# Fewer blocks with a dispatch of their own at the end of a hybrid attention and mixture-of-experts kernel

## The chip, the cores and the metric

The kernel runs on one core of a Trainium2 chip. The metric is the time of one execution in microseconds (us). Engines are named as in the profile: PE (matrix products; PEld its weight loads), DVE (vector), ACT (scalar), POOL (GpSimd, which also issues the indirect transfers) and SP (which issues most other transfers).

## The reference

The input is x of shape (4, 256, 64, 64) in float32. A first layer adds a local attention over 3x3 pixels. A second layer takes the pixels as tokens, 16384 of them with 256 channels, adds a gated mean over a window of 64 tokens, and then adds a mixture of eight experts of which each token uses two:

```python
x = x + conv_attention(group_norm(x))           # 3x3 neighbourhood
t = to_tokens(x)
t = t + windowed_mean(layer_norm(t))            # gate * x, window 64
# mixture of experts on tokens = layer_norm(t)
probs = softmax(tokens @ router_w.T)
rw, re = top_k(probs, 2); rw = rw / rw.sum(-1)
combine = zeros((N, 8)).at[arange(N)[:, None], re].set(rw)
out = tokens
for e in range(8):
    h = gelu(tokens @ w1[e] + b1[e])
    out = out + combine[:, e:e + 1] * (h @ w2[e] + b2[e])
x = from_tokens(t + out)
```

## The kernel before

**Blocks.** The 16384 tokens are cut into 32 blocks of 512 (`NB`; four rows of 128 each, `NT`). For each block the stages `attend`, `tail` and `produce` compute everything up to the mixture; `tail` leaves the normed tokens in a tile `tok` (pool `w3p`, tag `xl_tok`, three buffers) and the sum so far in a tile that is stored to `out`.

**Dispatch.** `ranks` gives each token and choice a row in a list of its expert in HBM (`rows_in`) and writes it there with indirect transfers on POOL (L1001): eight per block, each of 128 tokens. The first `NS` = 28 blocks are taken in groups (`GROUPS`: thirteen of two blocks, two of one). The last four blocks (`NB - NS`) form a lot of their own, named `APART`.

**Slots.** As soon as a group's rows are there, `experts` takes its full pieces of 256 rows of one expert as *slots*: four per block, less seven of the first group, 105 in all. For a slot SP fetches the rows (L1171, pool `rowp`, seven buffers), ACT copies the expert's first weights, PE transposes (L1195) and makes both products (L1207, L1225), ACT does the GELU, DVE adds the bias and scales (L1229, L1230), and POOL adds the result onto `out` with two accumulating indirect transfers (L1243), called *sums* here. A slot's sums wait until those of the slot before have landed, since one row may be in both. `give_rows` in `add` lets two or three of the waiting row transfers follow each slot's sums in POOL's order; rows that a fetch needs are given before it at the latest. The function `in_turn` fixes this order.

**Units.** What is left, the rests of the lists (`LEFT` = 21 pieces of 128 rows) and the last four blocks' rows (32 pieces), goes through `halves` as 53 *units* of 128 rows. The two kinds alternate as long as there are rests. Each unit is fetched by SP (L1319), transposed (L1334), multiplied (L1344, L1360), biased and scaled by DVE (L1371, L1372; L1364 first makes its row numbers in a tile with four buffers). Its result is then scattered by POOL into a table `sums_a` in HBM with a plain indirect transfer (L1373), one row for each token and choice, so that scatters need no order among themselves. Pieces of rests may also hold rows of earlier blocks; for these a sum onto `out` follows (L1390), again each behind the landing of the one before. `owed` holds sums that are not yet issued: each unit's scatter earns one credit, and a sum goes when its cost is there (1.5 for a unit's sum, 2.0 for one of the last `HELD` = 2 slots' pairs); with the last unit all that remain go.

**The end.** `together` reads, for the last four blocks, both choices' rows from `sums_a` (L1440, 512 KB a read, half by SP, half by ACT), adds them to the held sum on DVE (L1448) and stores it (L749).

**Order.** The main loop runs over the blocks; `follow` advances the slots' stream so that at the end of the blocks' work eleven, seven and three slots are left at fixed points. The last block's eight row transfers are made at once where `ranks` reaches them. Tiles in a pool take its buffers in turn, and a transfer into a buffer waits for its last reader.

Of the kernel before, what the change touches and what calls it, by code (L numbers as in the profile page):

```python
# [46 lines left out]
FP = mybir.dt.float32  # L47
# [5 lines left out]
P = 128  # L53
# [9 lines left out]
def hybrid_block_kernel(ctx: ExitStack, tc: tile.TileContext, ins: dict, out: bass.AP):  # L63
    nc = tc.nc
    x = ins["x"]
    B, C, FW, _ = x.shape
# [4 lines left out]
    NT = TB // P  # L71
    NBI = HW // TB
    NB = B * NBI
    E = ins["w1b"].shape[0]
# [15 lines left out]
    FETCH = 2  # L90
    I32, U32 = mybir.dt.int32, mybir.dt.uint32
    ENG = mybir.EngineType
    NS = NB - 4
    GROUPS = (*[2] * 13, *[1] * 2)
    assert sum(GROUPS) == NS
    first_of = [sum(GROUPS[:k]) for k in range(len(GROUPS))]
    where = [(k, j) for k, n in enumerate((*GROUPS, NB - NS)) for j in range(n)]
# [2 lines left out]
    U = 2  # L100
# [14 lines left out]
    RW = C + 2 * E  # L115
# [640 lines left out]
    def tail(g):  # L756
# [114 lines left out]
        if g < RAMP:  # L871
            scales()
        sent = t2
        if NS <= g < NS + 2:
            sent = xsp.tile([P, NC, TB], FP, tag="xs", name=f"held_{g}")
            sent = sent.rearrange("p c n -> p (c n)").rearrange("p (t c) -> p t c", t=NT)
        at = tc.cur_priority
# [76 lines left out]
    def ranks(g):  # L954
# [34 lines left out]
        def dispatch(inst):  # L989

            for i in range(k + 1):
                tc.declare_no_dep(
                    inst, group=f"dispatch_{i}", reason="no two tokens have one row"
                )
            tc.declare_no_dep(inst, group="fetch", reason="fetched rows are not written again")
            tc.add_to_no_dep_group(f"dispatch_{k}", inst)
            dispatched[k].append(inst)
            return inst
# [8 lines left out]

        for t in range(NT):
            for c in range(2):
                if g == NB - 1:  # L1010
                    dispatch(give(t, c).ins)
                elif g < first_of[2]:
                    waiting.append((k, lambda t=t, c=c: dispatch(paced(give(t, c)).ins)))
                else:
                    waiting.append((k, lambda t=t, c=c: in_turn(
                        dispatch(give(t, c).ins), adds[-1:], given_rows
                    )))
            yield
# [105 lines left out]

    ready = []
    adds = []
    HELD, owed = 2, []
    waiting, given_rows = [], []

    def in_turn(inst, others, own):  # L1130
# [17 lines left out]
    def experts():  # L1148
# [86 lines left out]
        def add(m, xs):  # L1235
            k, n = of[m]

            behind = adds[-U:]
            if n == 0:
                at = 1 + sum(GROUPS[:k])  # L1240
                behind = behind + stored[0 if k == 0 else at : at + GROUPS[k]]
            for t in range(U):
                inst = nc.gpsimd.indirect_dma_start(  # L1243
                    out=out, out_offset=bass.IndirectOffsetOnAxis(
                        ap=xs[:, t, C + E : C + E + 1].bitcast(U32), axis=0
                    ),
                    in_=xs[:, t, 0:C], in_offset=None, compute_op=ALU.add,
                ).ins
                tc.declare_no_dep(
                    inst, group="stores", keep=behind, reason="rows of a later group's blocks"  # L1250
                )
                tc.declare_no_dep(
                    inst, group="adds", keep=behind, reason="behind the slot before, no other"
                )
                for d in behind:
                    tc.add_manual_dep(
                        inst, d.name,
                        mybir.DependencyInfo(
                            mybir.DependencyClass.Sync, mybir.DependencyReason.DATA
                        ),  # L1260
                        reason="sums of one row",
                    )
                tc.add_to_no_dep_group("adds", inst)
                in_turn(inst, given_rows[-2:], [])
                adds.append(inst)
            give_rows(2 + (m % 3 == 0))

        raw = {m: fetch(m) for m in range(FETCH)}
        xcs, hs, done = {}, {}, {}
# [18 lines left out]
    def halves():  # L1288
# [10 lines left out]
            )  # L1299

        xs, w1s, xc, hs = {}, {}, {}, {}
        thirds, halved = [], []
        token = w1p.tile([P, HALVES], U32, tag="token", name="token")
        credit = 0.0

        def fetch(m):
            give_rows(0, APART)
            at = load(m, 1, [ENG.SP], E * ROOM)
            if order[m] < LEFT:
                if len(halved) == 0:  # L1310
                    both = rowp.tile([P, U, RW], FP, tag="xs", name=f"sxl_{m}")
                    halved.extend(both[:, n] for n in range(U))
                xs[m] = halved.pop(0)
            else:
                if len(thirds) == 0:
                    three = xp.tile([P, 3, RW], FP, tag="x", name=f"sxa_{m}")
                    thirds.extend(three[:, n] for n in range(3))
                xs[m] = thirds.pop(0)
            inst = nc.sync.dma_start(xs[m], rows_in[bass.ds(at, P), :]).ins  # L1319
            tc.add_to_no_dep_group("fetch", inst)  # L1320
            for d in dispatched[APART]:
                tc.add_manual_dep(
                    inst, d.name,
                    mybir.DependencyInfo(mybir.DependencyClass.Sync, mybir.DependencyReason.DATA),
                    reason="rows of the slot",
                )
# [27 lines left out]
        def output(m):  # L1354
            nonlocal credit
            e = load(m, 0, [ENG.PE, ENG.DVE], E - 1)
            h, x_ = hs.pop(m), xs.pop(m)
            ps = ps_a.tile([P, C], FP, tag="a", name=f"psya_{m}")
            for f in range(NC):
                nc.tensor.matmul(  # L1360
                    ps, h[:, f, :], w2[:, e, f, :], start=(f == 0), stop=(f == NC - 1)
                )
            to = w4p.tile([P, 1], U32, tag="to", name=f"to_{m}")
            nc.vector.tensor_tensor(  # L1364
                to, x_[:, bass.ds(e + C + E, 1)].bitcast(U32), spare[:, m : m + 1], ALU.max
            )
            if order[m] < LEFT:
                nc.vector.tensor_tensor(
                    token[:, m : m + 1], x_[:, bass.ds(e + C + E, 1)].bitcast(U32), beyond, ALU.min
                )  # L1370
            nc.vector.tensor_add(x_[:, 0:C], ps, b2b[:, e, :])  # L1371
            nc.vector.tensor_scalar_mul(x_[:, 0:C], x_[:, 0:C], x_[:, bass.ds(e + C, 1)])  # L1372
            inst = nc.gpsimd.indirect_dma_start(  # L1373
                out=sums_a[:, :], out_offset=bass.IndirectOffsetOnAxis(ap=to[:, 0:1], axis=0),
                in_=x_[:, 0:C], in_offset=None,
            ).ins
            tc.declare_no_dep(inst, group="sums", reason="one row for each token and choice")
            tc.add_to_no_dep_group("sums", inst)
            given_rows.append(inst)
            in_turn(inst, adds[-1:], [])  # L1380
            if order[m] < LEFT:
                owed.append((1.5, lambda: add(m, x_)))
            credit = credit + 1.0 if owed else 0.0
            while owed and (credit >= owed[0][0] or m == HALVES - 1):
                cost, sum_ = owed.pop(0)
                sum_()
                credit -= cost
# [33 lines left out]
    def together():  # L1421

        part = NT // 2
        for g in range(NS, NB):
            sums_of = None
            for n in range(0, NT, part):
                if g == NB - 1:
                    both = w3p.tile([P, NT, RW], FP, tag="xl_tok", name=f"both_{g}_{n}")
                    both = both.rearrange("p t r -> p (t r)")[:, 0 : 2 * part * C]
                    both = both.rearrange("p (t k c) -> p t k c", k=2, c=C)  # L1430
                elif g == NB - 2:
                    both = w2p.tile([P, NT, C + 1 + E], FP, tag="wx", name=f"both_{g}_{n}")
                    both = both.rearrange("p t r -> p (t r)")[:, 0 : 2 * part * C]
                    both = both.rearrange("p (t k c) -> p t k c", k=2, c=C)
                else:
                    if n == 0:
                        sums_of = xpp.tile([P, NT, 2, C], FP, tag="xp", name=f"both_{g}")
                    both = sums_of[:, n : n + part]
                first = OWN + 2 * ((g - NS) * TB + n * P)
                (nc.scalar if n else nc.sync).dma_start(  # L1440
                    both,
                    sums_a[first : first + 2 * part * P, :].rearrange(
                        "(t p k) c -> p t k c", p=P, k=2
                    ),
                )
                own = held[g][:, n : n + part]
                for k in range(2):
                    nc.vector.tensor_add(own, own, both[:, :, k, :])  # L1448
                store(g, own, n)
# [119 lines left out]
```

## Time and profile before

| what | value |
|---|---|
| median of three runs | 1240.46 us (1238.21 to 1243.04) |
| the profiled execution | 1240.63 us |
| its span, first to last instruction | 1238.9 us |
| PE, DVE, ACT, POOL busy | 90%, 74%, 69%, 57% of the span |
| row transfers L1001 | 256 of 0.995 us on average, 84.3 to 1056.8 us |
| slots' sums L1243 | 210 of 1.594 us, 188.0 to 1094.0 us |
| units' scatters L1373 | 53 of 0.96 us (median), 1082.4 to 1216.4 us |
| units' sums L1390 | 21 of 1.594 us (median), 1098.9 to 1200.0 us |
| reads of `sums_a` L1440 | 8 of 512 KB, from 1218.9 us |

Times on POOL are those of issuing the transfer; the transfer itself lands later. The idle time before an instruction is shown in brackets with what ended it. Of PE's products the ends are modelled, so its rows overlap a little.

### The profile page before, as it was taken

What the parts mean: (1) busy time and instruction counts of PE and PEld (TensorE: products, weight loads), DVE (VectorE), ACT (ScalarE), POOL (GpSimd) and SP (SyncE); (2) the same over time, 40 slices, a digit from 0 to 9 for tenths busy, and PEclk for the clock granted to TensorE, in tenths of its full rate; (3) what the DMA queues carried; (4) which work ended last, traced back from release to release, by engine and by line L of the source; (5) the groups of instructions that cost most, each with busy time, mean ns of one, the idle gap of its engine ahead of it and who ended that gap; (6) DMA issues with size and microseconds to landing.
All of it is one profiled execution on the core that took longest, in us unless ns stands there. A gap on an engine that the chain in (4) does not pass through costs nothing. (4 is left out here: it accounts for less than half of the span.)

```text
span 1238.9 us, 28986 instructions
## 1 busy us (share of the span) xinstructions
PE 1111.5 (90%) x8762; PEld 792.2 (64%) x8762; DVE 913.7 (74%) x4632; ACT 857.3 (69%) x1752; POOL 700.9 (57%) x642
## 2 busy tenths in 40 slices
PE   5988889999998979999999999999999999676882
PEld 3544456677675756777677666766766677565771
DVE  4589878888886867887988877888888887233344
ACT  1566679878886768787787787877877774344561
POOL 4013325666553655666655766665756577566671
PEclk7999999999998989999999999999999999889996
DMA  9894547666767667777766777766665456655446
GB/s 284 269 314 157 186 136 224 194 159 155 177 164 157 162 181 192 198 194 198 187 168 159 177 188 177 181 169 166 166 166 101 99 121 151 130 139 127 101 104 233
DMA packets 136145, 214.00 MB, mean 173 GB/s; under 512 B 16368, under 2 KB 102400, under 8 KB 131768
## 3 DMA queue, kind: packets, MB, share of 16 engines
q1 hardware_dynamic: 86264, 137.00, 35.8%
q0 software_dynamic: 48352, 73.05, 29.5%
q10 hardware_dynamic: 1376, 2.10, 0.5%
q8 instruction: 73, 1.20, 0.4%
q14 instruction: 80, 0.66, 0.2%
HBM read 120.78 MB, written 91.31 MB: 171 GB/s over the span
## 5 line engine op out<-in xcount | busy, mean ns | idle before, releaser
L1243 POOL DMA_INDIRECT out<-sx x210 | 334.7, 1594 | 273.5 <-DVE sx L1230 52.2
L1001 POOL DMA_INDIRECT rows_in<-tok,rows x256 | 254.6, 995 | 127.9 <-issue 78.4
L1225 PE MATMUL psy<-w,h 128*128 x840 | 213.2, 384 | 1.0 <-issue 0.6
L1207 PE MATMUL psh<-xc,w1s 128*128 128x256 f32 x840 | 205.4, 386 | 0.0
L1225 PEld LDWEIGHTS psy<-w,h 128*128 128x128 f32 x840 | 152.7, 190 | 51.3 <-issue 25.5
L1207 PEld LDWEIGHTS psh<-xc,w1s 128*128 128x128 f32 x840 | 152.8, 192 | 35.9 <-issue 10.6
L1229 DVE TENSOR_TENSOR sx<-psy,b2b 128x256 f32<-128x256 f32 x210 | 87.9, 419 | 57.1 <-PE psy L1225 52.3
L576 PE MATMUL psq<-x,qks 128*128 128x512 f32 x256 | 125.3, 612 | 1.8 <-ACT qks L497 1.8
L734 PE MATMUL pso<-mixT,vo 128*128 128x512 f32 x256 | 123.5, 605 | 0.0
L1213 ACT ACTIVATE h<-psh,w1s 128x256 f32<-128x256 f32 x210 | 88.2, 472 | 30.7 <-PE psh L1207 29.9
L1199 ACT COPY xc<-ptx 128x512 f32<-128x512 f32 x105 | 61.2, 583 | 37.0 <-PE ptx L1195 36.4
L1195 PE MATMUL ptx<-ident,sx 128*128 128x128 f32 x420 | 66.1, 280 | 20.8 <-DMA sx<-rows_in 20.7
L1195 PEld LDWEIGHTS ptx<-ident,sx 128*128 128x128 f32 x420 | 51.1, 146 | 46.0 <-issue 25.7
L1230 DVE TENSOR_SCALAR sx<-sx 128x256 f32<-128x256 f32 x210 | 75.5, 360 | 2.0
L1213 ACT ACT_TABLE_LOAD x59 | 75.7, 1283 | 0.8
L584 ACT ACTIVATE q<-psq,qbb,irc 128x512 f32<-128x512 f32 x64 | 49.9, 780 | 36.3 <-PE psq L576 29.6
L893 ACT ACTIVATE x<-x,scale 128x256 f32<-128x256 f32 x120 | 63.1, 590 | 16.8 <-DVE scale L867 13.0
L780 PE MATMUL psp<-wpr,x1c 128*128 128x136 f32 x512 | 70.2, 282 | 0.1
L576 PEld LDWEIGHTS psq<-x,qks 128*128 128x128 f32 x256 | 46.1, 194 | 35.5 <-issue 34.5
L835 PE MATMUL psw<-wx,band 128*64 128x512 f32 x128 | 68.8, 650 | 0.0
L832 PE MATMUL psw<-wl,bandl 128*64 128x512 f32 x128 | 68.8, 650 | 0.0
L780 PEld LDWEIGHTS psp<-wpr,x1c 128*128 128x128 f32 x512 | 65.5, 190 | 4.3 <-issue 2.1
(277 smaller groups left out, 2477.3 us busy)
## 6 DMA issues: line engine op xcount, KB each, us to landing
xp<-in_xp SPq DMA_DIRECT2D x32, 1024.0 KB
sx<-rows_in SPq DMA_DIRECT2D x105, 272.0 KB
x<-in_x SPq DMA_DIRECT2D x32, 660.0 KB
xs<-in_xs SPq DMA_DIRECT2D x32, 512.0 KB
out<-x SPq DMA_DIRECT2D x28, 512.0 KB
sxa<-rows_in SPq DMA_DIRECT2D x32, 136.0 KB
rows_in<-tok,rows POOLq DMA_INDIRECT x256
out<-sx POOLq DMA_INDIRECT x210
```

The source lines that it names most:

```text
L576: inst = nc.tensor.matmul(ps.rearrange("p (r w) -> p r w", w=W), qks[:, ci, co * P : (co + 1) * P], t[:, ci, 1 : TH + 1, 1 : W + 1], start ...
L734: nc.tensor.matmul(ps, vo[:, ci, co * P : (co + 1) * P], mixT[:, ci, :], start=(ci == 0), stop=(ci == NC - 1),)
L780: nc.tensor.matmul(ps[:, u, :], xc[:, ci, t * P : (t + 1) * P], wpr[:, ci, :], start=(ci == 0), stop=(ci == NC - 1),)
L832: one = nc.tensor.matmul(to[0:WIN], bandl, wl[part], start=True, stop=True)
L1001: return nc.gpsimd.indirect_dma_start(out=rows_in[:, :], out_offset=bass.IndirectOffsetOnAxis(ap=rows[:, c, t : t + 1], axis=0), in_=tok[: ...
L1195: nc.tensor.transpose(pt[:, c, t * P : (t + 1) * P], xs[:, t, c * P : (c + 1) * P], ident)
L1207: nc.tensor.matmul(ps[:, f, :], w1s[:, o : o + P], xc[:, ci, :], start=(ci == 0), stop=(ci == NC - 1),)
L1213: inst = nc.scalar.activation(h[:, f, :], ps[:, f, :], AF.Gelu, bias=w1s[:, F1 + f : F1 + f + 1])
L1225: nc.tensor.matmul(ps, h[:, f, t * P : (t + 1) * P], w2[:, e, f, :], start=(f == 0), stop=(f == NC - 1),)
L1229: nc.vector.tensor_add(ys[:, t, :], ps, b2b[:, e, :])
L1230: nc.vector.tensor_scalar_mul(ys[:, t, :], ys[:, t, :], xs[:, t, bass.ds(e + C, 1)])
L1243: inst = nc.gpsimd.indirect_dma_start(out=out, out_offset=bass.IndirectOffsetOnAxis(ap=xs[:, t, C + E : C + E + 1].bitcast(U32), axis=0), ...
```

## The change

It moves the border `NS` from 28 to 29: three blocks instead of four stay apart, and block 28 becomes a one-block group with four slots. There are thus 109 slots and 45 units (21 of rests, 24 of the three blocks). A unit's sum now costs 2.0 credits, and the last four slots' sums are held instead of two. After a slot's sums up to four waiting rows follow (four if more than four wait, else two). Of the last block's eight row transfers the first four are made at once and put into POOL's order ahead of the following sums; the other four join the waiting rows. The rests' units are fetched into tiles of four units in pool `w3p` (tag `xl_tok`) instead of tiles of two in `rowp`. In `together` blocks 29 and 30 read into pool `xpp`, block 31 into `xl_tok`.

```diff
-    NS = NB - 4
-    GROUPS = (*[2] * 13, *[1] * 2)
+    NS = NB - 3
+    GROUPS = (*[2] * 13, *[1] * 3)
...
-        if NS <= g < NS + 2:
+        if g == NS:
             sent = xsp.tile([P, NC, TB], FP, tag="xs", name=f"held_{g}")
...
         for t in range(NT):
             for c in range(2):
-                if g == NB - 1:
-                    dispatch(give(t, c).ins)
+                if g == NB - 1 and t < NT // 2:
+                    in_turn(dispatch(give(t, c).ins), [], given_rows)
                 elif g < first_of[2]:
...
-    HELD, owed = 2, []
+    HELD, owed = 4, []
...
-            give_rows(2 + (m % 3 == 0))
+            give_rows(4 if len(waiting) > 4 else 2)
...
             if order[m] < LEFT:
-                if len(halved) == 0:
-                    both = rowp.tile([P, U, RW], FP, tag="xs", name=f"sxl_{m}")
-                    halved.extend(both[:, n] for n in range(U))
-                xs[m] = halved.pop(0)
+                if len(fours) == 0:
+                    four = w3p.tile([P, NT, RW], FP, tag="xl_tok", name=f"sxl_{m}")
+                    fours.extend(four[:, n] for n in range(NT))
+                xs[m] = fours.pop(0)
...
             if order[m] < LEFT:
-                owed.append((1.5, lambda: add(m, x_)))
+                owed.append((2.0, lambda: add(m, x_)))
...
-                elif g == NB - 2:
-                    both = w2p.tile([P, NT, C + 1 + E], FP, tag="wx", name=f"both_{g}_{n}")
-                    both = both.rearrange("p t r -> p (t r)")[:, 0 : 2 * part * C]
-                    both = both.rearrange("p (t k c) -> p t k c", k=2, c=C)
                 else:
```

More of the change, by code (lines that the diff above doesn't have):

```diff
@@ L1301, in halves @@
         xs, w1s, xc, hs = {}, {}, {}, {}
-        thirds, halved = [], []
+        thirds, fours = [], []
         token = w1p.tile([P, HALVES], U32, tag="token", name="token")
```

## The prediction

> **What bounds the kernel now.** I read the busy time by stage first, because the averages of the page mix stages with different limits.
>
> ```profile
> 800.00:900.00 100.00, 99.52 (x809) 69.80 (x808) 83.09 (x444) 77.54 (x151) 62.28 (x52) 1.00 0.67 167
> ...
> 1058.00:1082.00 24.00, 16.10 (x96) 14.46 (x96) 4.00 (x14) 11.14 (x29) 12.32 (x8) 0.79 0.62 129
> 1082.00:1099.00 17.00, 10.01 (x56) 8.71 (x56) 4.48 (x17) 6.28 (x16) 12.38 (x12) 0.80 0.72 163
> 1099.00:1200.00 101.00, 77.21 (x497) 65.43 (x498) 37.74 (x124) 55.44 (x141) 66.65 (x56) 0.97 0.49 110
> 1200.00:1217.50 17.50, 14.20 (x96) 12.47 (x94) 8.47 (x27) 9.07 (x25) 12.16 (x12) 1.00 0.36 107
> 1217.50:1239.00 21.50, 0.00 (x0) 0.00 (x0) 9.99 (x16) 0.00 (x0) 0.00 (x0) 0.54 0.84 299
> ```
>
> The columns are the stretch, its length, busy time of PE, PEld, DVE, ACT and POOL, granted clock, DMA share and GB/s. Up to about 1036 us PE is the bound (99.5 of 100 us). Then come the units of 128 rows, where PE has a quarter of its time free, and from 1217.5 a tail of reads, sums and stores. Next the waits of POOL between 1099 and 1200:
>
> ```profile
> POOL out L1390 <- DMA out<-sxl,token: 20.3, 10, 3.5
> POOL sums_a L1373 <- issue: 8.2, 27, 0.3
> ```
>
> So POOL waits for almost nothing but the landing of the sum before. Its instructions in order of time show the pattern:
>
> ```profile
> 1104.49 1.57 POOL L1390 DMA_INDIRECT out<-sxl,token  x1 [2.66 <-DMA out<-sxl,token]
> 1106.37 0.98 POOL L1373 DMA_INDIRECT sums_a<-sxa,to  x1 [0.31 <-issue]
> 1107.65 0.96 POOL L1373 DMA_INDIRECT sums_a<-sxl,to  x1 [0.30 <-issue]
> 1108.91 1.60 POOL L1390 DMA_INDIRECT out<-sxl,token  x1 [0.30 <-issue]
> 1110.81 0.97 POOL L1373 DMA_INDIRECT sums_a<-sxa,to  x1 [0.30 <-issue]
> 1113.48 1.57 POOL L1390 DMA_INDIRECT out<-sxl,token  x1 [1.70 <-DMA out<-sxl,token]
> ```
>
> With one scatter (L1373) between two sums (L1390) the second waits; with two it doesn't. One scatter costs POOL 0.97 + 0.30 = 1.27 us, one sum 1.60 + 0.30 = 1.90 us.
>
> **Main stage: four slots more.** 105 slots become 109, 53 units become 45 (both 263 pieces of 128 rows). Bare, one slot takes PE 3.89 us, from one transpose to the next:
>
> ```profile
> 1036.96 0.60 PE L1195 MATMUL ptx<-ident,sx 128*128 128x128 f32 x4
> ...
> 1040.85 0.60 PE L1195 MATMUL ptx<-ident,sx 128*128 128x128 f32 x4
> ```
>
> The busy rows give more: (66.1 + 213.2 + 205.4) / 105 = 4.62, but the PE rows overlap, for they sum to more than PE's 1111.5. So four slots cost 15.6 to 18.5 us; I take 16.5. Their other work lies beside PE: eight sums of 1.90 us on POOL (62% busy there), four weight copies and eight GELUs on ACT (78%), sixteen DVE instructions of 0.35 to 0.42 us (83%), and a third one-block table, some fifteen DVE instructions of 0.15 to 0.4 us. If that cover were gone, POOL's 15 us would be the dearest. The store of block 28 (512 KB, one SP issue of 0.4 us) goes from the tail to this stage. Four rows per slot instead of two or three puts a block's eight rows behind three slots as 2, 4, 2; 2.6 us more of POOL before the next slot's sums, in a queue that has some 3 us of waiting per slot. It can shorten PE's waits for fetched rows before 1036 us (L1195, 20.7 us in all, 1.8 of it later), so this edit is worth 0 to -18.9 us. I count nothing: before 1036 us these are a few single stalls, the longest 8.2 us at 461, at places which a changed slot rate shifts.
>
> **From the last block's rows to the first unit's sum.** I walk POOL on before's clock and add the 16.5 at the end. The order of the changed program: four rows of the last block, two slots, two rows, a slot, two rows, a slot, two scatters, then four times a slot and two scatters, then the first unit's sum. Before: eight rows at 1047.92, four slots, two scatters, twice a slot and two scatters. A slot's sums wait for those of the slot before; in the trace they stand 6.6 us apart even with rows between (1017.57, 1024.38, 1030.93, 1037.50, 1044.21).
> - The row numbers are cast at 1034.18 and the tokens ready at 1035.2, so the four rows go at 1037.3, where a slot's sums stood, and end at 1042.4. Two slots at 1042.4 and 1049.0, done at 1052.8.
> - Two rows to 1055.3, slot at 1055.6, two rows to 1062.0, slot at 1062.2 to 1066.0. The last row starts at 1060.7 against 1056.83: 3.9 us later. Every unit's fetch waits for all these rows, and SP's queue stands behind them; the first goes 3.9 later too.
> - First unit scaled at 1070.9 in the trace, now 1074.8, the second 2.0 later. POOL idles from 1066 to 1074.8. Scatters to 1078.1, then held slots at 1078.1, 1084.7, 1091.3 and 1097.9 with two scatters each inside the 6.6, and the first unit's sum at 1104.5 (1098.94 before), with 10 scatters done instead of 6.
>
> Queued behind each waiting sum are the scatters; four unfinished ones stop DVE (L1364 has four buffers) and then PE, so units can't run ahead. The fetch of a fourth token tile (units 24 on) waits for four sums of the first one, which land at about scatter 18; PE has unit 24's transposes ahead of unit 22's product, so the margin is some two units, 5 us.
>
> **The units.** 21 sums remain, now strictly scatter, scatter, sum. POOL alone needs 2 x 1.27 + 1.90 = 4.44 us. The landing: ten sums with two or more scatters ahead of them let the next one start after 4.07 (twice), 4.56, 4.57, 4.62, 4.77, 4.96, 5.55, 5.73 and 6.37 us, mean 4.93; sums with one scatter ahead and two behind had landed four times out of four at 4.42. I take 4.8, nearer the first row, which has the two scatters ahead; bounds 4.44 and 5.05 (101.1 us over 20 intervals, the present mean). PE needs 1.97 us per unit (1073.77 to 1075.75), so it doesn't bound. From the first to the eighteenth sum: 17 x 4.8 = 81.6, thus 1186.1 on before's clock.
>
> The Trainium skill ("DMA: Bandwidth & Descriptors", "Anatomy of one DMA") fits 2.0 us plus bytes over 436 GB/s for such a transfer, an estimate of 2.3 us for 128 KB. The trace has 2.40 us from issue to landing for a scatter, but 3.85 and 4.78 for a sum, so the row decides; by the rule POOL's 4.44 would be the beat and the end 6 us earlier.
>
> **The tail.** Behind the eighteenth sum: a scatter (the last), then three sums alone, 19 to 21. The reads of the sums begin when the scatter lands. But the last of the six reads takes the fifth token tile's buffer (three buffers of `xl_tok`: three tokens, six token tiles, two tiles of reads), whose last reader is sum 20. From the eighteenth sum: 4.9 to sum 19, 4.9 to sum 20, 4.0 to its landing, 0.3 to ACT's issue, 3.3 for 512 KB alone, 1.5 for two DVE sums, 3.9 from there to the end (1234.97 to 1238.9): 22.8. Today's tail from the last scatter's end is 21.5. Without the chain it would be 1 MB shorter: eight reads took 9.98 us, six 7.5. That blocks 29 and 30 now read into other buffers, and one block less is held in `xsp`, changes no transfer. That the adds run beside five reads may cost them more; the bounds for the tail are 19 and 28 (two waits of 6.37 and 2 us more read).
>
> ```profile
> 1218.95 2.45 SPq L1440 DMA_DIRECT2D both<-sums_a  x4
> 1223.95 2.50 DVE L1448 TENSOR_TENSOR held<-held,both 128x512 f32<-128x512 f32 x4 [8.37 <-DMA both<-sums_a]
> ```
>
> The skill's same page ("Issuing engines are not separate DMA queues") speaks against the change here: transfers of all engines share 16 DMA engines, so the three sums and the reads take turns. The DMA share of 0.84 in the tail shows how little room there is, though no row has a sum beside such reads; if each landing doubled from 4 to 8 us the end would come 8 us later.
>
> **Sum.** 1186.1 + 16.5 + 22.8 = 1225.4 for the span against 1238.9. The profiled execution took 1240.63, 1.7 more than its span and 0.2 over the median of the three runs: 1227.1, say 1227 us, 1.1% less than 1240.46.
>
> **Rivals.**
> - *The gain goes into the sums' chain*: present mean beat 5.05 (85.9), full 18.5 for the slots, and the sums in the tail at the longest wait (+3.0): 1104.5 + 85.9 + 18.5 + 25.8 + 1.7 = 1236. For it: the units' stage would then still be one sum per 5.05 us. Against: four intervals with two scatters had no wait at all.
> - *Slower: a sum lands later behind two scatters each time.* Of the ten intervals the three longest average 5.88; with it for all 17: 100.0, and 1104.5 + 100.0 + 18.5 + 22.8 + 1.7 = 1247.5; with 6.37 for all, 1256. It decides from a beat of 5.84. For it: two of the three stand behind three scatters in a row. Against: slots with two rows or two scatters between kept 6.3 to 7.0.
> - *Better: the rows go earlier and PE's stalls before 1036 vanish.* Half of the 18.9 gives 1218, all 1208. For it: at 450 to 456 four rows stand together just before the stalled fetch. Against: PE lost almost nothing after 500 us with the old rule.
> - *The change doesn't do what it says*: POOL's order shows that the scatters do stand two to a sum; not counted.
>
> **Chances.** Forecast 0.55 (own range 1219 to 1234), better 0.17, gain eaten 0.18, slower 0.10. I take 1213 to 1241: the low end is three quarters of the stalls gone, the high end the eaten case with 5 us of late rows. A measurement tells about 0.5% (6 us) from no change: faster 0.72, same 0.18, slower 0.10.
>
> **What would show it.** Right: POOL in scatter, scatter, sum with waits under 0.5 us and a beat of 4.4 to 5.0; the first unit's sum some 22 us later than 1098.94; the last scatter some 14 us before 1216.4; last read issued alone on ACT after sum 20. Wrong: a beat above 5.5; POOL waiting on DVE in that stage (units too slow); a last row later than 1080; PE's stalls before 1050 much changed.

## The result, and the profile after

| kernel | median | runs | lowest to highest |
|---|---|---|---|
| before, on the same chip | 1241.75 us | 4 | 1238.21 to 1243.11 |
| after | 1267.97 us | 4 | 1265.72 to 1274.55 |

The ratio is 1.0243, with a 95% interval of 1.0204 to 1.0282: the change makes the kernel 2.4% slower (2.1% by the quotient of the two medians). The prediction was 1227 us, 1213 to 1241, so it was wrong in sign. The profiled execution of after has a span of 1265.9 us, 27.0 more than before's 1238.9.

The page of after: the first lines give the span and each engine's busy time, the two groups the busy time, the mean of one in ns, and the idle time ahead of them with what ended most of it.

```profile
span 1265.9 us, 28930 instructions
...
PE 1118.0 (88%) x8730; PEld 797.9 (63%) x8730; DVE 914.3 (72%) x4640; ACT 864.3 (68%) x1746; POOL 704.7 (56%) x642
...
L1225 PE MATMUL psy<-w,h 128*128 x872 | 221.3, 386 | 20.5 <-DVE sx L1229 19.7
...
L1195 PE MATMUL ptx<-ident,sx 128*128 128x128 f32 x436 | 69.2, 282 | 38.1 <-DMA sx<-rows_in 36.8
```

PE is busy for a smaller share of a longer span. It waits 36.8 us for fetched rows and once, for 19.7 us, ahead of a slot's second product. Before, the wait for fetched rows was 20.7 us:

```profile
L1195 PE MATMUL ptx<-ident,sx 128*128 128x128 f32 x420 | 66.1, 280 | 20.8 <-DMA sx<-rows_in 20.7
```

The wait of 19.7 us stands in the middle of the blocks' work, not at the end. The stretches of after (columns as in the prediction's first fence):

```profile
600.00:700.00 100.00, 78.91 (x574) 55.50 (x573) 70.34 (x349) 67.25 (x127) 54.15 (x45) 0.88 0.65 159
800.00:900.00 100.00, 99.92 (x813) 70.27 (x814) 81.78 (x420) 77.33 (x154) 62.03 (x52) 1.00 0.66 166
1119.00:1132.00 13.00, 7.62 (x37) 6.91 (x38) 1.42 (x6) 3.87 (x10) 2.71 (x2) 0.61 0.65 157
1132.00:1162.00 30.00, 25.12 (x173) 22.25 (x172) 11.01 (x38) 19.69 (x51) 22.51 (x18) 1.00 0.59 130
1162.00:1240.70 78.70, 63.16 (x422) 56.05 (x422) 33.62 (x114) 44.90 (x117) 60.25 (x52) 0.95 0.53 123
1240.70:1266.00 25.30, 0.00 (x0) 0.00 (x0) 7.49 (x12) 0.00 (x0) 7.27 (x5) 0.50 0.72 218
```

And the stretch of before that answers to the first of these lines:

```profile
600.00:700.00 100.00, 99.29 (x801) 69.71 (x801) 85.33 (x462) 78.84 (x158) 62.41 (x54) 1.00 0.68 165
```

Between 600 and 700 us all engines of after are slack and PE's granted clock is 0.88, while 800 to 900 is as dense as before. The units' stage and the tail are where the prediction looked; set against its milestones they carry almost none of the miss (span, us):

| leg | predicted | measured | miss |
|---|---|---|---|
| start to the last block's last row | 1077.2 | 1117.3 | +40.1 |
| last row to the first unit's sum | 43.8 | 44.7 | +0.9 |
| first to eighteenth sum | 81.6 | 78.7 | -2.9 |
| eighteenth sum to the end | 22.8 | 25.2 | +2.4 |

The four misses add up to 40.5, which is the whole distance from 1225.4 to 1265.9. What was to be found out is therefore why the blocks' work ends 40 us late.

Where PE stalls first, the traces read as follows. SP of after, in order of time:

```profile
604.18 0.38 SPq L1171 DMA_DIRECT2D sx<-rows_in  x1
604.66 0.41 SPq L152 DMA_DIRECT2D xp<-in_xp  x1
...
611.56 1.55 SPq L552 DMA_DIRECT2D xp<-mean_row  x2
613.21 0.41 SPq L165 DMA_DIRECT2D xs<-in_xs  x1
```

POOL, DVE and PE of after around it (the bracket is the idle time before an instruction and what ended it):

```profile
601.51 0.99 POOL L1001 DMA_INDIRECT rows_in<-tok,rows  x1 [0.30 <-issue]
...
616.91 0.69 DVE L179 BATCH_NORM_STATS2 stats<-xs 128x6 f32<-128x512 f32 x1 [25.84 <-DMA xs<-in_xs]
...
620.50 3.78 PE L1225 MATMUL psy<-w,h 128*128 x8 [19.69 <-DVE sx L1229]
```

The fetch at 604.18 (L1171) is that of slot 49, counted from 0, the first of the group of blocks 14 and 15. The last row that it needs is issued at 601.51. The fetch stands at the head of SP's queue, where SP waits 18.7 us for its rows, and goes as soon as that row has landed. Behind it in the same queue stand block loads: the edges (L552), which wait another 4.9 us for the load of `xp`, and the next block's `xs` (L165) go at 611.56 and 613.21. DVE, whose next instruction in program order is the statistics of that `xs` (L179), does nothing for 25.84 us; then PE waits for DVE. The same fetch in before, POOL's last row for it and then SP:

```profile
576.82 1.27 POOL L1001 DMA_INDIRECT rows_in<-tok,rows  x1 [0.30 <-issue]
...
582.91 0.38 SPq L1171 DMA_DIRECT2D sx<-rows_in  x1
583.39 1.54 SPq L552 DMA_DIRECT2D xp<-mean_row  x2
585.02 0.41 SPq L165 DMA_DIRECT2D xs<-in_xs  x1
```

There slot 49 is fetched at 582.91, 6.1 us after its last row is issued, and `xs` stands right behind it as well. SP waits for the rows here too, but 9.8 us, and DVE does not wait for `xs`. So the two kernels differ in how far a group's first fetch stands ahead of its rows, a thing that no line of the diff names. It is set in `follow`, which advances the slots to the lower of two lines:

```python
begins = [at + 2 + LAG for at in first_of[1:]] + [NS + 2.0]        # LAG = 0.35
most = [(at, max(0, n - FETCH - 1)) for at, n in ...]              # what is there
wanted = [(begins[1], 1), *((NB + n, first_slot[-1] - m) for n, m in ((0, 11), (1, 7), (2, 3)))]
```

`most` rises by four slots a block. `wanted` is a straight line from one slot at `begins[1]` = 6.35 blocks to the total less eleven at block 32. The total is now 109 instead of 105, with the same eleven left. Before, the line is (94 - 1) / 25.65 = 3.63 slots a block; after, (98 - 1) / 25.65 = 3.78. Where `wanted` is lower, the slots fall behind what is there: by 0.37 slots a block before and by 0.22 after. This reserve is added to the `LAG` of 0.35 blocks that a group's rows have to land before its first fetch is due. It also begins later: `wanted` is the lower line from block 14.4 on before (at 14.35 `most` is 30 and `wanted` 1 + 8 x 3.63 = 30.0), and in after only from 20.1 on (at 20.35 they are 54 and 1 + 14 x 3.78 = 53.9). Slot 49 is due at block 18.35 at the earliest, where before has a reserve and after has none. SP's waits of that kind (total us, times, longest) from 160 us to the end of the blocks, in after:

```profile
SPq L1171 <- DMA rows_in<-tok,rows: 155.9, 25, 18.8
```

Before it is:

```profile
SPq L1171 <- DMA rows_in<-tok,rows: 89.0, 17, 19.7
```

Nearly all of the difference comes after 500 us. From 500 to 700 us, in after:

```profile
SPq L1171 <- DMA rows_in<-tok,rows: 57.2, 7, 18.8
```

Before:

```profile
SPq L1171 <- DMA rows_in<-tok,rows: 19.7, 4, 9.3
```

From 700 to 1060 us before has no such wait, and after has 26.3 us.

### The profile page after: what moved, and what is told of

Read it like the earlier page. It is cut to its first block, busy times and chain, and to the rows that moved or that the text cites. A ratio compares the mean times of both kernels' runs of the same rounds, so it can differ in the third digit from the quotient of the medians.

```text
span 1265.9 us, 28930 instructions
## 1 busy us (share of the span) xinstructions
PE 1118.0 (88%) x8730; PEld 797.9 (63%) x8730; DVE 914.3 (72%) x4640; ACT 864.3 (68%) x1746; POOL 704.7 (56%) x642
## 5 line engine op out<-in xcount | busy, mean ns | idle before, releaser
L1243 POOL DMA_INDIRECT out<-sx x218 | 346.2, 1588 | 306.7 <-DVE sx L1230 30.7
L1225 PE MATMUL psy<-w,h 128*128 x872 | 221.3, 386 | 20.5 <-DVE sx L1229 19.7
L1207 PE MATMUL psh<-xc,w1s 128*128 128x256 f32 x872 | 215.6, 390 | 0.0
L1225 PEld LDWEIGHTS psy<-w,h 128*128 128x128 f32 x872 | 159.8, 191 | 75.1 <-issue 25.1
L1207 PEld LDWEIGHTS psh<-xc,w1s 128*128 128x128 f32 x872 | 159.9, 193 | 41.9 <-DVE x L855 6.5
L1229 DVE TENSOR_TENSOR sx<-psy,b2b 128x256 f32<-128x256 f32 x218 | 91.3, 419 | 56.9 <-PE psy L1225 40.3
L1195 PE MATMUL ptx<-ident,sx 128*128 128x128 f32 x436 | 69.2, 282 | 38.1 <-DMA sx<-rows_in 36.8
L1195 PEld LDWEIGHTS ptx<-ident,sx 128*128 128x128 f32 x436 | 53.8, 147 | 60.8 <-issue 41.9
L1230 DVE TENSOR_SCALAR sx<-sx 128x256 f32<-128x256 f32 x218 | 80.6, 370 | 2.5
L835 PE MATMUL psw<-wx,band 128*64 128x512 f32 x128 | 72.6, 679 | 0.0
L832 PE MATMUL psw<-wl,bandl 128*64 128x512 f32 x128 | 72.6, 679 | 0.0
L823 ACT COPY wl<-wx 64x795 f32<-64x795 f32 x32 | 27.2, 851 | 64.0 <-DVE wx L811 63.8
L576 PEld LDWEIGHTS psq<-x,qks 128*128 128x128 f32 x256 | 46.6, 195 | 36.8 <-issue 34.7
```

The costliest lines, as they stand in the source:

```text
L576: inst = nc.tensor.matmul(ps.rearrange("p (r w) -> p r w", w=W), qks[:, ci, co * P : (co + 1) * P], t[:, ci, 1 : TH + 1, 1 : W + 1], start ...
L832: one = nc.tensor.matmul(to[0:WIN], bandl, wl[part], start=True, stop=True)
L835: two = nc.tensor.matmul(to[WIN:P], band[:, WIN:P], wx[part], start=True, stop=True)
L1195: nc.tensor.transpose(pt[:, c, t * P : (t + 1) * P], xs[:, t, c * P : (c + 1) * P], ident)
L1207: nc.tensor.matmul(ps[:, f, :], w1s[:, o : o + P], xc[:, ci, :], start=(ci == 0), stop=(ci == NC - 1),)
L1225: nc.tensor.matmul(ps, h[:, f, t * P : (t + 1) * P], w2[:, e, f, :], start=(f == 0), stop=(f == NC - 1),)
```

## The experiments

Three parts of the change reach the blocks' work: the pace just worked out, the rule of up to four rows per slot, and the fourth slot group itself. The theory after the result was the pace, with the row rule as rival. In all experiments "after" and "before" are the two kernels of the result; ratios are to before on the same chip; after itself was timed for the result only, where before took 1241.75 us. PE's stalls are the gaps over 1 us that end between 160 and 1060 us, added up: 21.0 us before, 50.3 after. "Late" is how much later than in before the row numbers of block 31 are cast by DVE (L986): +53.8 us in after.

**Pace and rows, one at a time.** Four kernels.

`e1_old_pace`: after, with the pace of before (3.63).

```diff
-    wanted = [..., ((0, 11), (1, 7), (2, 3)))]
+    wanted = [..., ((0, 15), (1, 9), (2, 3)))]
```

> The changed kernel with the slots' pace of before (3.63 slots per block instead of 3.78: fifteen, nine and three slots left at the end of the blocks' work instead of eleven, seven and three). Theory P (the faster pace puts each group's first fetch earlier in SP's queue, where it waits for rows with the blocks' loads behind it): the stall of about 20 us near 620 us is gone, block 17's rows are numbered at most 10 us later than in the kernel before (40 us in the changed one), time 1228 to 1240 us. Theory R (up to four rows per slot delay the sums and so the fetches): stays near 1268.

`e2_before_new_pace`: before, with the pace of after (3.78).

```diff
-    wanted = [..., ((0, 11), (1, 7), (2, 3)))]
+    wanted = [..., ((0, 7), (1, 5), (2, 3)))]
```

> The kernel before with the changed kernel's pace alone (seven, five and three slots left instead of eleven, seven and three). Theory P: it loses 20 to 40 us in the blocks' stage, 1262 to 1282 us. Theory R: within 5 us of 1241.

`e3_old_rows`: after, with before's rule for rows; `e4_before_four_rows` is the reverse edit in before.

```diff
-            give_rows(4 if len(waiting) > 4 else 2)
+            give_rows(2 + (m % 3 == 0))
```

> The changed kernel with two or three rows per slot as before. Theory P: still slow, 1255 to 1285 us, with block 17's rows 25 us or more later than in the kernel before. Theory R: the stall is gone, 1228 to 1240 us.

> The kernel before with up to four rows per slot alone. Theory P: within 8 us of 1241, either sign. Theory R: 1260 us or more.

| kernel | median us | ratio (95%) | PE stalls | late |
|---|---|---|---|---|
| e1 after, old pace | 1238.51 | 0.9965 (0.9938 to 0.9991) | 26.3 | +16.1 |
| e2 before, new pace | 1276.67 | 1.0245 (1.020 to 1.029) | 45.9 | +48.2 |
| e3 after, old rows | 1257.17 | 1.0127 (1.0076 to 1.0177) | 42.8 | +43.5 |
| e4 before, four rows | 1250.57 | 1.0051 (1.0026 to 1.0077) | 25.7 | +9.7 |

The kernel before took 1242.58 here. The pace decides: undoing it takes 29.5 us off after (1267.97 - 1238.51), putting it alone into before adds 34.1. It also moves the same wait to the same place; DVE of e2 in order of time:

```profile
612.76 0.69 DVE L179 BATCH_NORM_STATS2 stats<-xs 128x6 f32<-128x512 f32 x1 [24.98 <-DMA xs<-in_xs]
```

The rows are a smaller cost of their own: 8.0 us in e4, 10.8 less in e3 than in after. Why four rows cost is less clear: PE's stalls grow by 5 us in e4 while SP's waits for rows stay (89.9 us against 89.0). With 1250.57 us e4 lies a little outside the 8 us around 1241 that the pace as the only cause allowed.

Not all that is late is lost. By block 32 `wanted` asks for 98 slots in after, e2 and e3 and for 94 in before, e1 and e4; four slots are some 16 us of PE by the prediction's price, work that comes earlier here and is missing later. So e2 is 48.2 us late there and 34.1 us longer in all.

**Without both, and the end without the border.** `e5_border_and_end` is after with the old pace and the old rule for rows (the edits of e1 and e3 together): the border, the price of 2.0, four sums held and the first rows ahead remain.

> The changed kernel with both the pace and the rows per slot of before: what is left of the change is the border (45 units, 109 slots), the held sums, the price of 2.0 and the first rows ahead. Theory P (pace and rows spoil the blocks' stage, the rest does what the prediction's sum said): 1224 to 1232 us, and about 10 us below the old pace alone. Rival (the end costs what it saves): 1236 to 1246.

`e7_before_new_end` comes from the other side: before, with the end alone (border, pace and rows as before, 53 units).

```diff
-                if g == NB - 1:
-                    dispatch(give(t, c).ins)
+                if g == NB - 1 and t < NT // 2:
+                    in_turn(dispatch(give(t, c).ins), [], given_rows)
...
-    HELD, owed = 2, []
+    HELD, owed = 4, []
...
-                owed.append((1.5, lambda: add(m, x_)))
+                owed.append((2.0, lambda: add(m, x_)))
```

and the rests' units in tiles of four, as in after.

> The kernel before with the end's edits alone: price 2.0, four slots held, first rows ahead, units of the rests in tiles of four; border, pace and rows per slot as before, so 53 units. By the prediction's beat of 4.63 us per two scatters and a sum with 12 scatters to spare at the end, 2 to 8 us less than before: 1234 to 1240. Rival (later rows cost more than the beat saves): 1242 to 1250.

`e8_rows_at_once` is e5 with all eight rows of the last block made at once, as before.

> As the run with border and end alone, but all eight of the last block's row transfers made at once as before. By the prediction's walk (the split delays the last row by 3.9 us): 2 to 6 us faster than that run. Rival: the same within 2 us, since slots' sums must go anyway.

Before took 1238.46 here. e5: 1229.13, 0.9929 (0.9896 to 0.9962). e7: 1228.47, 0.9916 (0.9884 to 0.9947). e8: 1226.98, 0.9886 (0.9827 to 0.9945). Their intervals overlap, so neither the border nor the first rows ahead is seen to do anything; what e5 and e7 share is faster than before. e7 gained more than was expected, and the gain expected of e8 (2 to 6 us below e5) is not resolved: its median is 2 us lower. PE's stalls are 23.0, 22.6 and 23.4 us. POOL of e5 at its first unit's sum:

```profile
1118.53 0.99 POOL L1373 DMA_INDIRECT sums_a<-sxl,to  x1 [0.30 <-DMA out<-sx]
1119.83 0.99 POOL L1373 DMA_INDIRECT sums_a<-sxa,to  x1 [0.30 <-issue]
1121.12 1.61 POOL L1390 DMA_INDIRECT out<-sxl,token  x1 [0.30 <-issue]
...
1125.71 1.60 POOL L1390 DMA_INDIRECT out<-sxl,token  x1 [0.30 <-issue]
```

The first unit's sum was predicted at 1121.0 and stands at 1121.12, with scatter, scatter, sum behind it.

**Is it the load behind the fetch?** The reading of the result's traces suggested that the harm is `xs` queued behind the waiting fetch. `e6_xs_on_act` is after with the later `xs` loads issued by ACT, whose queue has no such fetch.

```diff
-        nc.sync.dma_start(
+        (nc.sync if g < NBI else nc.scalar).dma_start(
```

> The changed kernel with the loads of the statistics' blocks (xs, after the first image) issued by ACT instead of SP. Theory Q (the stall of 25.8 us is this load standing in SP's queue behind fetches that wait for rows): DVE's wait for xs is gone, 18 to 27 us less than the changed kernel, 1241 to 1250. Rival (the rows themselves are late, any queue stalls): the wait only moves to another instruction, 1260 or more.

Measured: 1267.43 us, 1.0215 (1.0155 to 1.0276): nothing gained. The wait of DVE for `xs` is gone, and yet PE stalls 42.4 us and the stretch from 600 looks the same:

```profile
600.00:700.00 100.00, 82.95 (x613) 58.89 (x602) 67.49 (x345) 68.01 (x127) 57.36 (x48) 0.90 0.62 151
```

PE in the same stretch of e6 now waits for the fetched rows themselves:

```profile
615.12 1.09 PE L1195 MATMUL ptx<-ident,sx 128*128 128x128 f32 x4 [8.98 <-DMA sx<-rows_in]
```

SP still waits 170.9 us for rows in all. So that reading fell: `xs` was only the longest way by which the late fetch showed. The fetch has come due before its rows are there, and whatever needs it, or stands behind it, stalls.

**The fetch later, at a pace no slower.** If it is the reserve, then a later start of each group must do what a slower line does. `f1_later_fetch` is after with one number changed: each group's slots begin 0.3 blocks later, and the pace from there is (98 - 1) / 25.35 = 3.83, a little faster than that of after.

```diff
-    STEPS, LAG = {NB: 17, NB + 1: 12}, 0.35
+    STEPS, LAG = {NB: 17, NB + 1: 12}, 0.65
```

> Repeat on another chip: the changed kernel with the slots' stream started 0.3 of a block later behind each group's rows, its pace after that as fast as in the changed kernel. Theory Q2 (a group's first fetch stands in the queues before its rows have landed): PE's stalls of over 1 us between 160 and 1060 fall from 50 us to 25 or less, ratio to before 0.990 to 1.006. Rival (the faster pace is too much work for the blocks' stage): 1.012 or more.

`f2_middle_pace` is after with a pace between (3.70): knots (0, 13), (1, 8), (2, 3).

> Repeat on another chip: the changed kernel with 3.70 slots per block. Theory Q2: stalls between 26 and 50 us, ratio to before 0.998 to 1.018. Rival (a threshold: the single 20 us stall is there or not): within 0.004 of 0.9965 or of 1.0243.

f1: 1245.16 us, 0.9996 (0.9967 to 1.0025), 22.8 less than after. Its stalls are 19.7 us, and SP waits for rows a third as long as in after:

```profile
SPq L1171 <- DMA rows_in<-tok,rows: 50.6, 18, 8.3
```

f2: 1246.36 us, 1.0017 (0.9984 to 1.005); stalls 36.9, late +34.1: between e1 and after in each. SP's waits for rows at L1171 after 500 us (total us):

| kernel | 500 to 700 us | 700 to 1060 us |
|---|---|---|
| before | 19.7 | none |
| e1 after, old pace | 16.6 | none |
| f1 after, later fetch | 18.7 | 14.6 |
| f2 after, middle pace | 36.1 | 1.9 |
| e2 before, new pace | 43.9 | 11.3 |
| after | 57.2 | 26.3 |

So a group's start relative to its rows is the cause, by two different edits, and not a pace that is too much work for the blocks' stage: the pace of f1 is the fastest in the table. f1 is still 28.9 us late. By the prices above that is mostly four slots' work (some 16) and the row rule (9.7 in e4), an estimate.

**Price and hold alone; and a pace slower still.** `f3_price_and_hold` is before with two numbers changed, `HELD` 4 and the price 2.0.

> Repeat on another chip: the kernel before with the price of 2.0 and four held slots alone. If they make the gain of the new end by themselves: ratio 0.986 to 0.995. If the held slots' buffers stop the units' fetches: 0.997 or more.

`f4_slower_pace` is e7 with knots (0, 13), (1, 8), (2, 3), which is (92 - 1) / 25.65 = 3.55 slots a block.

> Repeat on another chip: the kernel before with the new end and 3.55 slots per block. Theory Q2: fewer stalls than the 21 us of before and a ratio of 0.980 to 0.992, at most that of the new end alone. Rival (the late slots' sums delay the units): 0.994 or more.

f3: 1225.55 us, 0.9853 (0.980 to 0.9905). f4: 1219.58 us, 0.9818 (0.9773 to 0.9864), the shortest time in this study and faster than both kernels. In f4 the row numbers of block 31 come 12.3 us *earlier* than in before, although its stalls (23.3) are no smaller, where fewer were expected. In f3 the price and the hold by themselves give the whole gain of the new end: more than e7's 0.9916, though the intervals overlap. In both, with all 53 units, the last sum goes about when it did (1197.1 us in e7 and 1197.3 in f3, 1200.0 before) and the last scatter some 15 us earlier (1201.5 and 1201.8, against 1216.4). The border, the tiles of four and the rows ahead are not needed for it. That f4 is faster than f3 is likely from the medians and not shown by the intervals.

**The same on two other chips.** Four of these edits had also run on a chip on which before took 1277.04 us, and two more on one with 1273.91; there only the ratios can be used.

> The changed kernel with the slots' stream started 0.3 of a block later behind each group's rows (LAG 0.65 instead of 0.35); the pace after that is as fast as in the changed kernel (3.83 slots per block). Theory Q2 (not the work is too much but a group's first fetch stands in the queues before its rows have landed): PE's stalls of over 1 us between 160 and 1060 fall from 50 us to 25 or less, time 1232 to 1248 us. Rival (the faster pace loads POOL, ACT or DVE more than the blocks' stage can carry): 1258 us or more.

> The changed kernel with a pace in between (3.70 slots per block; thirteen, eight and three slots left). Theory Q2: the fetches gain reserve earlier, so the stalls lie between those of the old pace (26 us) and of the changed one (50 us), time 1240 to 1262 us. Rival (a threshold: the single 20 us stall is either there or not): within 4 us of 1238 or of 1268.

> The kernel before with the price of 2.0 and four held slots alone: rows at once as before, and the rests' units still in tiles of two in the pool of the slots' rows. If price and hold make the gain of the new end by themselves: 1226 to 1234 us. If the held slots' buffers stop the units' fetches, so that the tiles of four are needed: 1236 us or more.

> The kernel before with the new end, and a pace slower than before (3.55 slots per block; thirteen, eight and three left). Theory Q2: less stall in the blocks' stage, but two slots more behind it, where PE is free a quarter of the time: 1220 to 1230 us, at most the 1228 of the new end alone. Rival: the late slots' sums delay the units, 1232 or more.

`g1_slowest_pace` is e7 with knots (0, 15), (1, 9), (2, 3), 3.47 slots a block; `g2_price_hold_slower` is f3 with f4's pace.

> The kernel before with the new end and 3.47 slots per block (fifteen, nine and three slots left). If reserve is all that counts: stalls no more than the 23 us at 3.55 and a ratio of 0.978 to 0.984. If the slots that are left over now delay the units: 0.986 or more.

> The kernel before with the price of 2.0, four held slots and 3.55 slots per block; the rows at once and the tiles of two as before. If price, hold and pace are the whole gain: ratio 0.978 to 0.986, the same as with the whole new end at this pace. If the first rows ahead and the tiles of four are needed too: 0.988 or more.

| kernel | same edit as | ratio (95%) |
|---|---|---|
| e9 | f1 | 1.0043 (1.0008 to 1.0077) |
| e10 | f2 | 1.0133 (1.0061 to 1.0206) |
| e11 | f3 | 0.9827 (0.9747 to 0.9906) |
| e12 | f4 | 0.9805 (0.9735 to 0.9874) |
| g1 | e7, 3.47 | 0.982 (0.9738 to 0.9902) |
| g2 | f3, 3.55 | 0.9839 (0.9753 to 0.9925) |

The order of e9 to e12 is that of f1 to f4, with wider intervals. PE's stalls are not to be compared across the chips: e9 has 26.9 us, where at most 25 were expected, and e10 only 14.7, where 26 to 50 were, and no trace of before was taken there. Whether a pace below 3.55 gives more, and whether f4 needs more than f3 with its pace, stays open.

## Why the prediction was wrong

**The step that failed** is the working of "Main stage: four slots more": it counted four slots at 16.5 us and the change in slot rate at nothing. The one bound that it set on PE's stalls there, "worth 0 to -18.9", was for the row rule and allowed a gain or nothing; of the stalls it said that they were "at places which a changed slot rate shifts". It saw that the rate changes and did not work out by how much or which way: 3.63 to 3.78 slots a block, with which the reserve of a group begins to grow at block 20.1 instead of 14.4, and by 0.22 instead of 0.37 slots a block. That "PE lost almost nothing after 500 us with the old rule" was true and was used only against a larger gain. It was the reserve of the old pace that made it so: SP's waits for rows fell to 19.7 us between 500 and 700 us and to none behind. In after PE loses 4.0 and 19.7 us at 535 and 620. The pace costs 29 to 34 us (e1, e2).

**The second mis-sized term** is the row rule, also counted at nothing: 8 to 11 us (e4, e3). These two hold the whole miss; e5, which undoes both, takes 1229.13 us where 1227 was forecast. This agreement is in part luck: e5 leaves fifteen slots after block 32 instead of eleven, so its last row comes at 1071.7 (1077.2 predicted), the first unit's sum 49.4 us later instead of 43.8, and the two misses cancel; the other two legs are 80.0 (81.6) and 25.9 (22.8). Nor does it show that the border pays, as the forecast had it: e7 and f3 have the old border and are as fast, by the price and the held sums alone.

**What held.** POOL stands in scatter, scatter, sum; in after its waits from 1162 to 1241 (total, times, longest) are:

```profile
POOL out L1390 <- issue: 5.2, 14, 0.6
...
POOL out L1390 <- DMA out<-sxl,token: 1.6, 3, 0.8
```

Before, the second of these was 20.3 us. The beat is (1240.7 - 1162.0) / 17 = 4.63 us, inside 4.4 to 5.0 and below the 4.8 taken; from one sum to the next, in order of time:

```profile
1166.48 1.60 POOL L1390 DMA_INDIRECT out<-sxl,token  x1 [0.30 <-issue]
1168.39 0.98 POOL L1373 DMA_INDIRECT sums_a<-sxl,to  x1 [0.30 <-DVE sxa L1371]
1169.67 0.96 POOL L1373 DMA_INDIRECT sums_a<-sxa,to  x1 [0.30 <-issue]
1171.10 1.60 POOL L1390 DMA_INDIRECT out<-sxl,token  x1 [0.46 <-issue]
```

So the rivals that went by the beat (5.05 and above 5.84) did not happen, and "slower" came from a place that no rival named. Of the listed signs two spoke at once: a last row later than 1080 (1117.3), and PE's stalls before 1050 much changed.

**The tail** was 25.2 us instead of 22.8. POOL, ACT and DVE of after behind the eighteenth sum:

```profile
1240.69 1.60 POOL L1390 DMA_INDIRECT out<-sxl,token  x1 [0.30 <-issue]
...
1244.72 1.57 POOL L1390 DMA_INDIRECT out<-sxl,token  x1 [1.14 <-DMA out<-sxl,token]
1245.09 12.55 ACTq L1436 DMA_DIRECT2D both<-sums_a  x3
1253.22 1.57 POOL L1390 DMA_INDIRECT out<-sxl,token  x1 [6.93 <-DMA out<-sxl,token]
1257.40 1.56 POOL L1390 DMA_INDIRECT out<-sxl,token  x1 [2.61 <-DMA out<-sxl,token]
1260.91 1.90 DVE L1444 TENSOR_TENSOR x<-x,both 128x512 f32<-128x512 f32 x3 [4.09 <-DMA both<-sums_a]
```

From sum 19 to sum 20 it takes 8.50 us, with five reads of 512 KB issued beside it; from 18 to 19 (4.03) no read has been issued yet, and from 20 to 21 (4.18) none is issued until 1257.3. ACT's issues end at 1257.6 with the last read, just behind the landing of sum 20 that lets sum 21 go, as predicted from the buffers. The Trainium skill ("DMA: Bandwidth & Descriptors", "Issuing engines are not separate DMA queues") says that transfers of all engines interleave on the same 16 DMA engines; the forecast quoted it and priced the sums without it at 4.9. The trace fits the page here: this one landing about doubled, though not all three, and it made 3.6 of the tail's 25.2 us (8.50 - 4.9).

**What stays open.** The stalls of after at 464, 535 and 620 us (12.0, 4.0 and 19.7) follow the first fetches of three groups in turn, at 459.75, 531.36 and 604.18. The next three, at 682.74, 755.37 and 814.10, also go only when their rows land, SP waiting up to 18.0 us, and yet PE has no stall from 625 to 1032 us; why is not settled. The cost of the row rule is measured and not followed to its cause.

## What to carry to other kernels

Where one count sets the slope of a schedule, a change of the count is a change of the pace everywhere: work out the new slope and the distance between a producer and its first consumer at each place before counting the work itself. A stage whose waits are short has a reserve that makes them short, and an edit to its rate needs a bound on the side of a loss too. A transfer that waits at the head of an in-order queue holds up loads that have nothing to do with it; moving one of them away (e6) gained nothing, asking later (f1) 23 us.

## What the hardware showed besides

A stall costs PE's clock as well: with 19.69 us idle at once, the granted clock over 600 to 700 us was 0.88. It was 1.00 in the first 3.8 us of that stall (600.8 to 604.6), 0.51 in the 23.9 us that followed, 8.0 of them after PE had work again, and 0.99 from 628.5 to 640. The Trainium skill ("TensorE: Matmul & The Clock Gate", "What's actually happening") says that an idle window of about 3.4 us sets the clock to half and a busy one sets it free again; the 3.8 us before the clock fell fit that.

The same program, before, has a median of 1238 to 1243 us in four of its measurements here and of 1274 and 1277 on two other chips, a difference as large as the one under study.
